# A two-layer graph network on one core: the order of the first loads, the dummy products, and the last result in three pieces

## The chip, the core and the metric

The kernel runs on one core of a Trainium2 chip. Five engines work beside each other, each through its own list of instructions in order: TensorE (PE in the profile, its weight loads PEld), VectorE (DVE), ScalarE (ACT), GpSimd (POOL) and SyncE (SP, which only issues transfers). ScalarE and GpSimd issue transfers too, each through its own queue. The metric is device microseconds of the whole program, and one number stands for a kernel: the median of several runs. All times below are in microseconds unless marked ns.

## The reference

Thirty-two graphs of 512 nodes with 128 features share one 512x512 adjacency of zeros and ones. Layer 0 is graph attention, layer 1 a gated recurrence of five steps; each is added to its input.

```python
h = jnp.maximum(_layernorm(x, axis=-1), 0.0)
x = x + _L0_gnn_ref(h, adj, W, b, a_src, a_dst)
h = jnp.maximum(_layernorm(x, axis=-1), 0.0)
x = x + _L1_gnn_ref(h, adj, adj, w3_w, ..., u5_b, 5)

# layer 0
h = einsum('bnf,fc->bnc', x, W)
logits = leaky_relu((h @ a_src)[:, :, None] + (h @ a_dst)[:, None, :], 0.2)
alpha = softmax(logits + mask, axis=-1)
out = leaky_relu(einsum('bij,bjc->bic', alpha, h) + b, 0.3)

# layer 1, one step (in_matrix and out_matrix are both adj)
m_in = einsum('nm,bmd->bnd', in_matrix, h);  m_out = einsum('nm,bmd->bnd', out_matrix, h)
av = concatenate([m_in, m_out], axis=-1);    u3 = h @ u3_w.T + u3_b
z = sigmoid(av @ w3_w.T + w3_b + u3);        r = sigmoid(av @ w4_w.T + w4_b + u3)
hv = tanh(av @ w5_w.T + w5_b + (r * h @ u5_w.T + u5_b))
h = (1.0 - z) * h + z * hv
```

## The kernel before

**A plan made on the host.** While the program is built, every piece of work becomes a `Task` with an engine, an estimated length, a key (its due time), the tasks that it needs, the buffers that it takes, and `lands`, the time until its result is seen. `plan` (L107) then walks through simulated time and picks for each engine the task with the lowest key among those that could begin, and the instructions are recorded in that order. So each engine's order is fixed by these estimates: `STORE_LANDS` and `SPREAD_LANDS` (L69) are the times allowed for a store or a load on GpSimd's queue, `CROSSED` (L70) the one for a transposing transfer, `ADJ_LANDS` (L38) the one for the adjacency. `SHIFT` (L48) moves single tasks' keys by parts of a step. `EARLY` and `LEVEL` (L35) say for how many graphs the pace of the due times differs at the start and at the end. `BRANCH` (L71) is how many tasks stand behind the load of a flag, which every engine reads to decide whether a general path has to run; here it never does.

**The first loads.** ScalarE's queue issues gw (the layer's 128x128 weight) and the two score vectors, one row each (L430 to L432). SP issues x of graph 0, the adjacency `a_sb` (1 MB), x of graphs 1 and 2, and the other weights (L449 to L454). TensorE turns gw (L476), multiplies the two score rows by a one to make columns of them (L487), and multiplies gw with these columns (L496). Four small ScalarE copies (L501 to L504) put the result beside gw into `wrow`, so that one product per tile (`hp`, L866) gives both the features and the scores.

**Dummies.** `idle` (L462) is a product of constants. Its tasks have a key behind everything, so the plan puts them where TensorE would have nothing else: the first `FIRST_IDLE` of 480 units from 500 ns on, the other `IDLE` of 256 units from 6500 ns on.

**Layer 0** of a graph: the norm's statistics and the relu on DVE, GpSimd and ScalarE; the turned activations (`h0T`, by TensorE for the first four graphs, later by 32x32 blocks on DVE and a trip through DRAM that GpSimd issues, L793 and L806); `hp`; exponentials of the scores on ScalarE; `es`, the scores of all nodes along the free axis; the weights `pt` (L981, DVE), which need `es` and a block of the transposed adjacency `adjT`; the averages `av` (L1013); the addition of x (`join`, L1066); and the second norm. `adjT` is made by TensorE turns (L527) and a copy per block (L534), block 3's on DVE (`BY_DVE`). Graph 3's `join` runs on GpSimd (`JOIN_POOL`).

**Layer 1.** Each state lives transposed (`hT`, times 4096) and as two f16 halves `hi` and `lo` with nodes on the partitions. A step on TensorE: eight f16 products with `adjT` (`m`, L1129), then five f32 products of 512 columns: g (L1148, L1149), z (L1169), v (L1192, L1193). Each f32 product stands in the profile as two records. ScalarE makes the tanh of each, DVE three combinations (L1206, L1212, L1215). The crossing to the next step (`crossed`, L1326): ScalarE casts `hT` to f16, DVE takes the rest, and SP issues a transposing transfer for each (L1340). The first step's `hT` comes by the DRAM trip (`turn_b`). Up to ten graphs are under way, which covers the crossing's latency with other graphs' products.

**The end.** The last four graphs' results are turned by TensorE. For the last two (`near`) the kept part is made ahead: graph 30's by ScalarE (`lowered`, L1219), DVE (`keep`, `gated_hv`) and GpSimd (`twice`, L1231). Graph 31's last step is `ending` (L1351), in `PIECES` of two 128-column tiles each: tanh, two DVE instructions, turns, the result, and a store per piece on the queue that `STORES` names. The constants `plus` and `minus` (0.5 and -0.5/4096 times the identity) are made but not used.

Of the kernel before, what the change touches and what calls it, by code (L numbers as in the profile page):

```python
# [15 lines left out]
P = 128  # L16
# [18 lines left out]
EARLY = 6  # L35
LEVEL = 9
EARLY_NORMS = ("a1", "a2", "a3", "b0")
ADJ_LANDS = 5600  # L38
HALVED = 1
BY_DVE = (3,)  # L40
JOIN_POOL = (3,)
LOW_POOL = ()
UNSCALED = 1
PIECES = (2, 2)
STORES = ('ACT', 'SP')
ENDING_KEY = 0
Z_AHEAD = 0
SHIFT = {  # L48
    ('adj', 2): 0.13, ('adj', 3): 1.0, (0, 1, 'step'): 3.5, (0, 12): 1.5, (1, 2, 'step'): -1.5,
    (1, 9): 1.85, (2, 0, 'step'): 3.0, (2, 1, 'step'): 1.5, (2, 15): 6.0, (2, 18): 1.0,  # L50
    (2, 2, 'step'): -0.08, (2, 9): -2.0, (25, 1, 'step'): 1.0, (25, 2, 'step'): -0.5,
    (25, 4, 'step'): -3.5, (26, 2, 'step'): 8.5, (27, 4, 'step'): -1.5, (29, 1, 'step'): 1.5,
    (29, 3, 'step'): -0.55, (29, 4, 'step'): -3.0, (3, 0): -0.5, (3, 0, 'step'): 1.0,
    (3, 15): 3.0, (3, 18): 5.5, (3, 26): 1.84, (3, 5): -3.0, (3, 9): -1.23, (30, 3, 'step'): -0.5,
    (30, 4, 'step'): -4.0, (31, 3, 'step'): -2.27, (4, 9): 2.0,
# [11 lines left out]
FIRST_IDLE, IDLE = 32, 36  # L67
LANDING = 5000
STORE_LANDS, SPREAD_LANDS = 3500, 5000  # L69
CROSSING, CROSSED = 1250, 1400  # L70
BRANCH = 150  # L71
# [236 lines left out]
def gat_then_gated_gnn_kernel(  # L308
# [40 lines left out]
    def add(*args, **kwargs):  # L349
        tasks.append(Task(*args, **kwargs))  # L350
        return tasks[-1]
# [53 lines left out]
    avecs = prep.tile([1, 2, D], F32, name="avecs")  # L405
# [3 lines left out]
    unlift = const.tile([P, 1], F32, name="unlift")  # L409
    nc.vector.memset(unlift, -1 / LIFT)  # L410
# [9 lines left out]
    def load_x(b, key=None, lands=3000):  # L420
        f = Buffer("x")

        def issue():
            pin(nc.sync.dma_start(out=new(f, f"x_{b}", (P, K, D)), in_=x_r[b]))

        needs = () if key else (bias_loaded,)
        load = add("SP", [1], key or 5 * (b - LEAD) * STEP, issue, needs, (f,), lands=lands)
        return f, load

    nc.scalar.dma_start(out=gw, in_=g_w)  # L430
    nc.scalar.dma_start(out=avecs[:, 0, :], in_=g_asrc.rearrange("(o d) -> o d", o=1))
    nc.scalar.dma_start(out=avecs[:, 1, :], in_=g_adst.rearrange("(o d) -> o d", o=1))  # L432
# [17 lines left out]
    a_loaded = add("SP", [1], -9.8e9, lambda: load_rest("a"), lands=ADJ_LANDS)  # L450
    xs[1] = load_x(1, -9.7e9, 5000)
    xs[2] = load_x(2, -9.6e9, 5100)
# [15 lines left out]
    for i in range(FIRST_IDLE + IDLE):  # L468
        add("PE", [480 if i < FIRST_IDLE else 256], 1e12, idle, (), (f_idle,),
            at=500 if i < FIRST_IDLE else 6500)  # L470
# [6 lines left out]
            at=4000)  # L477
# [6 lines left out]
    def issue():  # L484
        new(f_ac, "ac_ps")
        for i in range(2):
            pin(nc.tensor.matmul(  # L487
                f_ac.tile[:, i : i + 1], lhsT=avecs[0:1, i, :], rhs=ones[0:1, 0:1], start=True,
                stop=True,
            ))  # L490

    u = add("PE", [256] * 2, soon, issue, (), (f_ac,), at=4100)
    u = add("ACT", [1], soon, lambda: pin(nc.scalar.copy(acols, f_ac.tile[:, 0:2])), (u,), (f_ac,))

    def issue():
        pin(nc.tensor.matmul(new(f_wa, "wa_ps")[:, 0:2], lhsT=gwT, rhs=acols, start=True, stop=True))  # L496

    t = add("PE", [256], soon, issue, (u, t), (f_wa,), at=4800)

    def issue():  # L500
        pin(nc.scalar.copy(wrow[:, D : D + 1], f_wa.tile[:, 1:2]))  # L501
        pin(nc.scalar.mul(wrow[:, D + 1 : D + 2], f_wa.tile[:, 0:1], 0.8))
        pin(nc.scalar.mul(wrow[:, D + 2 : D + 3], f_wa.tile[:, 1:2], -0.8))
        pin(nc.scalar.copy(wa, f_wa.tile[:, 0:2]))  # L504
# [318 lines left out]
    def layer0(b):  # L823
# [7 lines left out]
        def keys(i):  # L831
            return begin + length * (base[0] + i) / parts + SHIFT.get((b, base[0]), 0) * STEP
# [168 lines left out]
        def o():  # L1001
            return f_o.tile or new(f_o, f"o_{b}", (P, K, D))
# [63 lines left out]
        def join(ks):  # L1066
            pin((nc.gpsimd if by_pool else nc.vector).tensor_tensor(x1[:, ks, :], f_x.tile[:, ks, :], o()[:, ks, :], ALU.add))

        by_pool = False
        if by_halves:  # L1070
            joined = []
            for part, ks in enumerate((slice(0, K // 2), slice(K // 2, K))):
                t = add("DVE", [256], keys(0.3 * part), lambda ks=ks: leak(ks), averaged[part : part + 1],
                        (f_o,))
                joined.append(add("DVE", [256], keys(0.3 * part), lambda ks=ks: join(ks), (t,),
                                  (f_o, f_x)))
        else:
            t = add("DVE", [512], keys(0), lambda: leak(slice(0, K)), averaged, (f_o,))
            by_pool = b in JOIN_POOL
            joined = [add("POOL" if by_pool else "DVE", [512], keys(0), lambda: join(slice(0, K)),  # L1080
                          (t, finished.get(b - SLOTS)), (f_o, f_x), ns=1350 if by_pool else None)]
# [13 lines left out]
    def halves(b, src, key, needs, buffers, order="p k d -> p k d", **sizes):  # L1095
        hi = his[b % SLOTS].rearrange(order, **sizes)
        lo = los[b % SLOTS].rearrange(order, **sizes)

        def low():
            pin((nc.gpsimd if by_pool else nc.vector).tensor_tensor(lo, src(), hi, ALU.subtract))  # L1100

        by_pool = b in LOW_POOL

        high = add("ACT", [480], key, lambda: pin(nc.scalar.copy(hi, src())), needs, buffers)
        return high, add("POOL" if by_pool else "DVE", [512], key, low, (high,), buffers,
                         ns=1350 if by_pool else None)


    def recurrence(b, step, halved, turned):
# [109 lines left out]
        def lowered():  # L1219
            pin(nc.scalar.activation(  # L1220
                new(f_kept, f"less_{b}"), f_z.tile, AF.Identity, bias=unlift, scale=1 / LIFT
            ))

        def keep():
            pin(nc.vector.tensor_tensor(new(f_d, f"kept_{b}"), f_kept.tile, hT, ALU.mult))
# [5 lines left out]
        def twice():  # L1231
            pin(nc.gpsimd.tensor_tensor(f_d.tile, f_hv.tile, f_d.tile, ALU.subtract))

        if near:
            f_kept = Buffer("r")
            t_keep = add("ACT", [512], keys(4), lowered, (t_z,), (f_z, f_kept))
            t_keep = add("DVE", [512], keys(3.5) - STEP, keep, (t_keep,), (f_kept, f_d))
            t = add("DVE", [512], keys(5), gated_hv, (t, t_z), (f_z, f_hv))
            turned = add("POOL", [512], keys(5), twice, (t, t_keep), (f_hv, f_d), ns=1400)
            to_turn = f_d  # L1240
        else:
            t = add("DVE", [512], keys(5), differ, (t,), (f_hv, f_d))
            t = add("DVE", [512], keys(5), gated, (t, t_z), (f_z, f_d))
            turned = add("DVE", [512], keys(5), update, (t,), (f_d,))
            to_turn = None
# [66 lines left out]
        def result_at_once():  # L1312
            pin(nc.vector.scalar_tensor_tensor(
                new(f_res, f"res_{b}", (P, K, D)), src(), 0.5 if near else 1 / LIFT,
                x1s[b % SLOTS], ALU.mult, ALU.add,
            ))
# [34 lines left out]
    def ending(b, keys, t_rh, t_z, buffers):  # L1351
# [13 lines left out]
        def piece(i, ks):  # L1365
            f = Buffer("o", "bank") if i else f_v
            of = slice(ks.start * P, ks.stop * P)
# [14 lines left out]
            def gated():  # L1382
                hv = f_hv.tile[:, of]
                pin(nc.vector.scalar_tensor_tensor(
                    hv, f_z.tile[:, of], 1.0, hv, ALU.add, ALU.mult
                ))
                pin(nc.vector.scalar_tensor_tensor(
                    f_d.tile[:, of], hv, LIFT, f_d.tile[:, of], ALU.mult, ALU.subtract
                ))

            def turn():
                for k in range(ks.start, ks.stop):
                    pin(nc.tensor.transpose(
                        f.tile[:, ts(k - ks.start, P)], f_d.tile[:, ts(k, P)], ident
                    ))

            def result():
                res = f_res.tile or new(f_res, f"res_{b}", (P, K, D))
                pin(nc.vector.scalar_tensor_tensor(
                    res[:, ks, :], f.tile[:, :width].rearrange("p (k d) -> p k d", d=D),  # L1400
                    0.5 / LIFT, x1s[b % SLOTS][:, ks, :], ALU.mult, ALU.add,
                ))
# [10 lines left out]
            u = add("DVE", [width] * 2, keys(4 + key), gated, (u, t_z, t_keep), (f_z, f_hv, f_d))  # L1413
            u = add("PE", [256] * (ks.stop - ks.start), keys(4 + key), turn, (u,), (f, f_d))
            u = add("DVE", [width], keys(5 + key), result, (u,), (f, f_res))
# [66 lines left out]
```

## Time and profile before

| | us |
|---|---|
| median of 5 runs | 1138.51 |
| lowest and highest | 1136.83, 1139.75 |
| profiled execution, its time | 1137.72 |
| profiled execution, its span | 1136.0 |
| TensorE busy in it | 1127.9 |
| DVE, ACT, POOL busy | 874.2, 666.7, 359.9 |

The span runs from the program's first instruction to its last. The time of an execution is 1.7 longer than its span. A product of 512 columns in f32 is recorded as two matmuls of 592 ns, which start 429 ns apart when they follow each other, and one in f16 as one of 379 ns with 216 ns to the next; so records overlap, and where one asks what TensorE was held up by, the distance from start to start says more than the busy time.

### The profile page before, as it was taken

The numbers are of one execution on the slowest core, as the hardware profiler recorded it, in microseconds if no ns is written. First come the engines' busy times: TensorE is split into PE (matmuls) and PEld (weight loads), VectorE is DVE, ScalarE is ACT, GpSimd is POOL, SyncE is SP. The second block draws the span as 40 slices with busy tenths as digits, with TensorE's granted clock in tenths as the row PEclk, the third lists the DMA queues.
The fourth block names the chain that finished last, engine by engine and source line by source line (L and its number), as shares of the span: only waits on it lengthen the run. The fifth ranks groups of instructions, "written<-read, shape, count | busy, mean of one in ns | idle before, by whom it ended". The sixth has DMA issues, their size and how long they took to land.

```text
span 1136.0 us, 14339 instructions
## 1 busy us (share of the span) xinstructions
PE 1127.9 (99%) x4318; PEld 591.1 (52%) x4318; DVE 874.2 (77%) x2007; ACT 666.7 (59%) x1302; POOL 359.9 (32%) x516
## 2 busy tenths in 40 slices
PE   9999999999999999999999999999999999999998
PEld 7555554555455544555544555555555554444444
DVE  7978868787777778787787887798887976647555
ACT  6666656555655566565566565666665555545553
POOL 4446614331430344322344322545453130100000
DMA  3345526464435446444455444555564343322222
GB/s 107 75 103 112 111 57 112 88 125 84 108 82 95 97 106 108 90 92 107 93 108 100 88 100 107 102 121 113 111 121 87 63 93 56 74 47 70 69 65 68
DMA packets 188629, 105.56 MB, mean 93 GB/s; under 512 B 152066, under 2 KB 167556, under 8 KB 188420
## 3 DMA queue, kind: packets, MB, share of 16 engines
q1 hardware_dynamic: 170368, 66.57, 25.9%
q0 software_dynamic: 17888, 37.84, 18.3%
q8 instruction: 35, 0.57, 0.2%
q14 instruction: 46, 0.38, 0.1%
q10 hardware_dynamic: 292, 0.20, 0.1%
HBM read 39.98 MB, written 30.99 MB: 62 GB/s over the span
## 4 chain that ended last, share of the span: by engine, by line
PE 93%; DVE 3%; DMA 2%; ACT 1%; POOL 1%; issue 1%; ACTq 0%; DVEq 0%; POOLq 0%
PE m L1129 23%; PE g L1148 12%; PE g L1169 12%; PE g L1149 12%; PE v L1193 11%; PE v L1192 11%; PE av L1013 9%; PE hp L866 2%; DVE pt L981 1%; DMA turn_b<-blocks_b 1%; DMA hi<-hiT 0%; PE idle L463 0%; DMA hT<-turn_b 0%; DMA avecs<-in_L_gnn_a_dst_dram 0%; DVE st_a L656 0%
## 5 line engine op out<-in xcount | busy, mean ns | idle before, releaser
L1206 DVE SCALAR_TENSOR_TENSOR d<-hv,hT 128x512 f32<-128x512 f32 x158 | 108.4, 686 | 112.5 <-ACT hv L1199 111.7
L1154 ACT ACTIVATE rs<-g,zrb 128x512 f32<-128x512 f32 x160 | 109.9, 687 | 119.3 <-PE g L1149 117.6
L1199 ACT ACTIVATE hv<-v,vb 128x512 f32<-128x512 f32 x159 | 108.9, 685 | 116.2 <-PE v L1193 115.9
L1148 PE MATMUL g<-hT,u3T 128*128 128x512 f32 x320 | 163.6, 593 | 1.1 <-DMA hT<-turn_b 1.1
L1129 PE MATMUL m<-adjT,hi 128*128 128x512 f16 x640 | 162.9, 379 | 1.7 <-DMA hi<-hiT 1.7
L1149 PE MATMUL g<-mT,w4sT 128*128 128x512 f32 x320 | 163.4, 592 | 0.0
L1169 PE MATMUL g<-mT,w3dT 128*128 128x512 f32 x320 | 162.5, 592 | 0.0
L1192 PE MATMUL v<-mT,w5sT 128*128 128x512 f32 x318 | 162.4, 592 | 0.0
L1193 PE MATMUL v<-rh,u5hT 128*128 128x512 f32 x318 | 162.4, 592 | 0.0
L1129 PE MATMUL m<-adjT,lo 128*128 128x512 f16 x640 | 162.0, 379 | 0.0
L1161 DVE SCALAR_TENSOR_TENSOR rh<-rs,hT 128x512 f32<-128x512 f32 x160 | 109.5, 686 | 53.1 <-ACT rs L1154 48.8
L685 POOL TENSOR_TENSOR rs_b<-ve_b,mhalf 128x4 f32<-128x4 f32 x32 | 37.5, 1173 | 349.4 <-DVE ve_b L665 209.6
L1181 ACT ACTIVATE zs<-g,zrb 128x512 f32<-128x512 f32 x160 | 109.8, 686 | 62.1 <-PE g L1169 61.6
L1013 PEld LDWEIGHTS av<-hw,pt 128*128 128x128 f32 x1024 | 124.4, 191 | 23.4 <-issue 18.7
L1140 ACT COPY mT<-m 128x512 f32<-128x512 f32 x160 | 93.3, 584 | 73.0 <-PE m L1129 70.4
L1013 PE MATMUL av<-hw,pt 128*128 128x129 f32 x1024 | 126.1, 275 | 0.2 <-DVE pt L981 0.2
L1332 ACT CAST hiT<-hT 128x512 f16<-128x512 f32 x128 | 78.8, 616 | 72.1 <-DVE hT L1215 72.0
L1215 DVE SCALAR_TENSOR_TENSOR hT<-d,hT 128x512 f32<-128x512 f32 x158 | 109.3, 692 | 13.0 <-PE v L1192 0.5
L1129 PEld LDWEIGHTS <-hi 128*128 128x128 f16 x640 | 62.5, 98 | 106.0 <-issue 52.8
L1212 DVE SCALAR_TENSOR_TENSOR d<-zs,d 128x512 f32<-128x512 f32 x158 | 109.3, 692 | 5.2
L1129 PEld LDWEIGHTS <-lo 128*128 128x128 f16 x640 | 62.4, 98 | 91.0 <-issue 24.9
L1149 PEld LDWEIGHTS g<-mT,w4sT 128*128 128x128 f32 x320 | 60.8, 190 | 76.5 <-issue 70.8
(148 smaller groups left out, 1384.2 us busy)
## 6 DMA issues: line engine op xcount, KB each, us to landing
x<-in_x_dram SPq DMA_DIRECT2D x32, 256.0 KB, 2.9
out_dram<-res SPq DMA_DIRECT2D x31, 256.0 KB, 2.2
turn_b<-blocks_b POOLq DMA_DIRECT2D x120, 64.0 KB, 2.8
hT<-turn_b POOLq DMA_DIRECT2D x30, 256.0 KB, 3.6
turn_a<-blocks_a POOLq DMA_DIRECT2D x112, 64.0 KB, 2.9
h0T<-turn_a POOLq DMA_DIRECT2D x28, 256.0 KB, 3.7
es<-line POOLq DMA_DIRECT2D x28, 256.0 KB, 4.2
way<-blocks SPq DMA_DIRECT2D x28, 256.0 KB, 2.0
```

The lines of the kernel that those rows point to most:

```text
L1013: pin(nc.tensor.matmul(avs()[:, i, :], lhsT=f_pts[c].tile[:, ts(2 * part + i, P)], rhs=hw()[:, c, : D + 1], start=start, stop=(c == K - 1) ...
L1129: pin(nc.tensor.matmul(f_m.tile, lhsT=part[:, k, :], rhs=adjT[:, k, :], start=(first and k == 0), stop=(not first and k == K - 1),))
L1148: pin(nc.tensor.matmul(g, lhsT=u3T, rhs=hT, start=True, stop=False))
L1149: pin(nc.tensor.matmul(g, lhsT=w4sT, rhs=f_mT.tile, start=False, stop=True))
L1154: pin(nc.scalar.activation(new(f_r, f"rs_{b}_{step}"), f_g.tile, AF.Tanh, bias=rb, scale=0.5))
L1161: pin(nc.vector.scalar_tensor_tensor(new(f_rh, f"rh_{b}_{step}"), f_r.tile, 1.0, hT, ALU.add, ALU.mult))
L1169: pin(nc.tensor.matmul(f_g.tile, lhsT=w3dT, rhs=f_mT.tile, start=False, stop=True, skip_group_check=True))
L1181: pin(nc.scalar.activation(new(f_z, f"zs_{b}_{step}"), f_g.tile, AF.Tanh, bias=zb, scale=0.5))
L1192: pin(nc.tensor.matmul(v, lhsT=w5sT, rhs=f_mT.tile, start=True, stop=False))
L1193: pin(nc.tensor.matmul(v, lhsT=u5hT, rhs=f_rh.tile, start=False, stop=True))
L1212: pin(nc.vector.scalar_tensor_tensor(d, f_z.tile, 1.0, d, ALU.add, ALU.mult))
L1215: pin(nc.vector.scalar_tensor_tensor(hT, f_d.tile, 0.5, hT, ALU.mult, ALU.add))
```

## The change

- The score vectors become two partitions of one tile, are loaded ahead of gw on ScalarE's queue, and are turned by one TensorE transpose. The product with gw gets each column 32 times (64 columns, 32 of each score).
- SP loads x of graph 1 ahead of the adjacency.
- All adjacency blocks are copied by ScalarE; no join is on GpSimd.
- 24 + 32 dummies where there were 32 + 36; the second kind is shorter in the plan (190 units) and may begin at 5500.
- Graph 30's kept part is made by DVE alone.
- Graph 31's result comes in pieces of 2, 1 and 1 tiles, stored by SP, ScalarE, ScalarE. The first piece (`BY_MATMUL`) is turned by products with `minus` (the kept part, early) and `plus` (the gated part) that add up in PSUM.
- Estimates, `SHIFT`, `EARLY`, `LEVEL` and `BRANCH` are others, and with them the order of all engines. In TensorE's order of the new kernel the 56 dummies stand among the start's products, the last one in graph 0's second step, and none after it; in the old one 33 stand in the start and 35 among the last products.

```diff
-EARLY = 6
-LEVEL = 9
+EARLY = 7
+LEVEL = 8
-ADJ_LANDS = 5600
+ADJ_LANDS = 5650
-BY_DVE = (3,)
-JOIN_POOL = (3,)
-LOW_POOL = ()
+BY_DVE = ()
-PIECES = (2, 2)
-STORES = ('ACT', 'SP')
-ENDING_KEY = 0
+PIECES = (2, 1, 1)
+STORES = ('SP', 'ACT', 'ACT')
+ENDING_KEY = -4
+BY_MATMUL = (0,)
 SHIFT = {
...
-FIRST_IDLE, IDLE = 32, 36
+FIRST_IDLE, IDLE = 24, 32
-STORE_LANDS, SPREAD_LANDS = 3500, 5000
+STORE_LANDS, SPREAD_LANDS = 4000, 5500
-BRANCH = 150
+BRANCH = 110
...
-    avecs = prep.tile([1, 2, D], F32, name="avecs")
+    avecs = prep.tile([2, D], F32, name="avecs")
...
+    nc.scalar.dma_start(out=avecs[0:1, :], in_=g_asrc.rearrange("(o d) -> o d", o=1))
+    nc.scalar.dma_start(out=avecs[1:2, :], in_=g_adst.rearrange("(o d) -> o d", o=1))
     nc.scalar.dma_start(out=gw, in_=g_w)
-    nc.scalar.dma_start(out=avecs[:, 0, :], in_=g_asrc.rearrange("(o d) -> o d", o=1))
-    nc.scalar.dma_start(out=avecs[:, 1, :], in_=g_adst.rearrange("(o d) -> o d", o=1))
...
-    a_loaded = add("SP", [1], -9.8e9, lambda: load_rest("a"), lands=ADJ_LANDS)
-    xs[1] = load_x(1, -9.7e9, 5000)
-    xs[2] = load_x(2, -9.6e9, 5100)
+    xs[1] = load_x(1, -9.8e9, 3700)
+    a_loaded = add("SP", [1], -9.7e9, lambda: load_rest("a"), lands=ADJ_LANDS)
+    xs[2] = load_x(2, -9.6e9, 6000)
...
-        add("PE", [480 if i < FIRST_IDLE else 256], 1e12, idle, (), (f_idle,),
-            at=500 if i < FIRST_IDLE else 6500)
+        add("PE", [480 if i < FIRST_IDLE else 190], 1e12, idle, (), (f_idle,),
+            at=500 if i < FIRST_IDLE else 5500)
...
-        for i in range(2):
-            pin(nc.tensor.matmul(
-                f_ac.tile[:, i : i + 1], lhsT=avecs[0:1, i, :], rhs=ones[0:1, 0:1], start=True,
-                stop=True,
-            ))
+        pin(nc.tensor.transpose(new(f_ac, "ac_ps")[:, 0:2], avecs, ident[0:2, 0:2]))
...
-        def lowered():
-            pin(nc.scalar.activation(
-                new(f_kept, f"less_{b}"), f_z.tile, AF.Identity, bias=unlift, scale=1 / LIFT
-            ))
         def keep():
-            pin(nc.vector.tensor_tensor(new(f_d, f"kept_{b}"), f_kept.tile, hT, ALU.mult))
+            pin(nc.vector.scalar_tensor_tensor(
+                new(f_d, f"kept_{b}"), f_z.tile, -1.0, hT, ALU.add, ALU.mult
+            ))
...
         def twice():
-            pin(nc.gpsimd.tensor_tensor(f_d.tile, f_hv.tile, f_d.tile, ALU.subtract))
+            pin(nc.vector.scalar_tensor_tensor(
+                f_d.tile, f_hv.tile, LIFT, f_d.tile, ALU.mult, ALU.subtract
+            ))
...
+            def turn_kept():
+                new(f_end, f"end_{b}_{i}")
+                for k in range(ks.start, ks.stop):
+                    pin(nc.tensor.matmul(
+                        f_end.tile[:, ts(k - ks.start, P)], lhsT=f_d.tile[:, ts(k, P)], rhs=minus,
+                        start=(k == ks.start), stop=False, skip_group_check=True,
+                    ))
+
             def turn():
                 for k in range(ks.start, ks.stop):
-                    pin(nc.tensor.transpose(
-                        f.tile[:, ts(k - ks.start, P)], f_d.tile[:, ts(k, P)], ident
-                    ))
+                    if by_matmul:
+                        pin(nc.tensor.matmul(
+                            f_end.tile[:, ts(k - ks.start, P)], lhsT=f_hv.tile[:, ts(k, P)],
+                            rhs=plus, start=False, stop=True, skip_group_check=True,
+                        ))
+                    else:
+                        pin(nc.tensor.transpose(
+                            f.tile[:, ts(k - ks.start, P)], f_d.tile[:, ts(k, P)], ident
+                        ))
...
+            n = ks.stop - ks.start
+            if by_matmul:
+                kept = add("PE", [512] * n, keys(-1), turn_kept, (t_keep, pieces[0]), (f_end, f_d))
+                u = add("DVE", [width], keys(4 + key), gated, (u, t_z), (f_z, f_hv))
+                u = add("PE", [512] * n, keys(4 + key), turn, (u, kept), (f_end, f_hv))
+            else:
+                u = add("DVE", [width] * 2, keys(4 + key), gated, (u, t_z, t_keep),
+                        (f_z, f_hv, f_d))
+                u = add("PE", [256] * n, keys(4 + key), turn, (u,), (f, f_d))
+            u = add("DVE", [width], keys(5 + key), result, (u,), (f_end, f_res))
```

## The prediction

> **What bounds the kernel now.** I read the busy line first, then the chain of waits over the whole span, the waits by engine, the busy time by stretches, and at last the chain and the timeline of both ends.
>
> ```profile
> PE 1127.9 (99%) x4318; PEld 591.1 (52%) x4318; DVE 874.2 (77%) x2007; ACT 666.7 (59%) x1302; POOL 359.9 (32%) x516
> ...
> PE 93%; DVE 3%; DMA 2%; ACT 1%; POOL 1%; issue 1%; ACTq 0%; DVEq 0%; POOLq 0%
> ```
>
> TensorE is the bound, but busy time counts filling instructions, so I asked for stretches:
>
> ```profile
> 0.00:26.00 26.00, 24.09 (x181) 20.88 (x182) 19.69 (x93) 17.29 (x56) 9.59 (x24) 1.00 0.35 117
> 60.00:340.00 280.00, 280.00 (x1057) 145.75 (x1057) 223.37 (x521) 168.80 (x331) 107.75 (x151) 1.00 0.49 98
> 352.00:1094.00 742.00, 742.00 (x2751) 380.59 (x2751) 570.74 (x1257) 432.29 (x822) 222.13 (x316) 1.00 0.44 92
> 1126.00:1136.00 10.00, 6.70 (x50) 5.29 (x48) 4.92 (x9) 1.48 (x3) 1.26 (x1) 1.00 0.18 58
> ```
>
> After the window come its length and the busy time of PE, weight loads, DVE, ACT, POOL. From 60 to 340 and from 352 to 1094 TensorE has not one gap, and both kernels put the same products there. The change can win or lose only in the first 60 us, in single stalls, and in the last 10 us. The stalls are two:
>
> ```profile
> PE m L1129 <- DMA hi<-hiT: 1.7, 1, 1.7
> PE g L1148 <- DMA hT<-turn_b: 1.1, 1, 1.1
> ```
>
> By start-to-start distances, longer than a pair's usual 0.43 and 0.22, they cost 1.82 us at 52.5 and 1.29 us at 347.6. The ends:
>
> ```profile
> 1.77 4.40 DMA avecs<-in_L_gnn_a_dst_dram
> ...
> 6.21 0.38 PE ac_ps L487 x2
> ```
>
> ```profile
> 1126.48 1.26 POOL L1232 TENSOR_TENSOR kept<-hv,kept 128x512 f32<-128x512 f32 x1 [137.64 <-DVE hv L1229]
> 1126.57 1.73 DVE L1359 SCALAR_TENSOR_TENSOR kept<-zs,hT 128x512 f32<-128x512 f32 x1 [0.17 <-ACT zs L1181]
> ...
> 1130.85 0.38 ACTq L1406 DMA_DIRECT2D out_dram<-res  x1
> 1131.18 1.51 SPq L1406 DMA_DIRECT2D out_dram<-res  x1
> ```
>
> At the start a 512-byte row of the score vectors takes 4.40 us and holds TensorE until 6.21. At the end a DVE instruction that takes 0.69 elsewhere takes 1.73 beside GpSimd's, the last issue on SP takes 1.51 against 0.33 of its like, and the span ends 4.8 us after that issue began.
>
> **The start.** The ScalarE queue issued at 0.74, 1.26 and 1.77. The score rows now take the first two places and gw the third. The third row took 4.40 because it came behind the adjacency's 8 KB packets, whose records run from 3.1 to 5.6; gw in the first place took 3.2. So gw lands between 1.77 + 3.2 = 4.9 and 1.77 + 4.4 = 6.2. I take 4.9: x of graph 1 (256 KB) now goes ahead of the adjacency, which at the 390 GB/s of these packets puts off the adjacency by 0.67, to begin near 3.7, while gw's packets, 1.66 after the issue as in the old first place, come at 3.43. From gw on: turn to copy 0.45, copy 0.27, product and four copies as from 6.87 to 7.61, 0.74, so wrow is whole at 6.4, not 7.61. The adjacency lands at 6.36 + 0.67 = 7.0, and its first turn, at 7.96 before since it stood behind wrow's work, starts at 7.05. The two score columns cost one transpose for two products, nothing beside the wait.
>
> What follows is ScalarE and DVE. ScalarE now casts the fourth adjacency block too (BY_DVE empty; 0.6 more on ScalarE, 0.68 less on DVE, nothing else). From its first cast's end, 7.05 + 0.68 + 0.59 = 8.32, stand the exponentials 0.80, scaling 1.15, two casts 1.20, two relus 0.8 and the fourth cast 0.6: 12.9. The two last weighings at 0.415 end at 13.7; they ended at 14.54. From there to the bias of graph 1's second norm (33.41) DVE worked 18.87 us; the new order has one mean and variance pair and one small product less on this stretch (0.7). So this bias comes 0.8 to 1.5 us earlier, and the first aggregation of graph 1 with it, with the same TensorE work before it (26.4 us of products by pitch in both orders). If gw lands late, only DVE's 0.7 is left, or nothing. I take -1.1, bounds -1.5 and 0.
>
> Of the dummies (0.11 each) 56 now lie in the start and none at the end; before it was 33 and 35. Eighteen run during the first load. The 22 that are new, 2.4 us, stand where TensorE waits for ScalarE's copies and DVE's weighings; that wait is their cover, and without it they cost up to +2.4. I take 0. Without dummies in the end, the turns of the last pieces follow each other within 0.9 us, as the 0.76 and 0.22 us gaps there do now.
>
> The clock column above reads 1.00 in every stretch, but the dummies' own rows do not: 0.213 us apart up to 4.36, 0.11 from 6.5 on. The Trainium skill, TensorE: Matmul & The Clock Gate, section Part 1: The HAM clock gate, says that an idle window of about 3.4 us halves the clock. By it the end without dummies would stay at full rate, its gaps being shorter, and at half rate the six turns would cost 0.11 more each, 0.7; no trace here shows such a gap.
>
> Against the new place of gw speaks DMA: Bandwidth & Descriptors, section Queues, rings and completion order: an engine drains a whole packet of one queue's descriptors before it turns to the next queue. The row agrees (the late row moved at 5.40, when the adjacency was nearly through). By the rule everything hangs on which comes first, and coming second would make the start's term -0.7 or less.
>
> **The ramp and its crossings.** Each step's state goes from TensorE's v over ScalarE, three DVE steps, a cast and SP's transposing DMA back to m. I added the pitches of the products that stand between in each order. Before, graph 1 step 1 had 7.8 us and needed 9.78: the stall of 1.82. Needed in the ramp: 7.45 to 10.4, the contended two 9.78 and 9.68; after 1000 us: 6.3 to 6.7. The new order gives 7.4 (graph 4 step 3), 8.0 (1, 1), 8.6 (0, 2), 8.8 (0, 1), 8.8 (3, 1), where the old gave 7.8, 8.3, 8.8, 9.1, and 10.4 for (3, 1). At most 1.8 is saved; if (3, 1) and (4, 3) wait 0.9 and 1.0 more, it is +1.9. Nearest is the old row for (1, 1) again with a little more for (3, 1): +0.3. Late, the least is 7.7, as before, where the slack was 1.0 to 1.5; there the flag's load (0.55 on DVE, 0.47 on ScalarE, 0.51 on SP) now stands beside graph 29 step 4's crossing with a slack of 1.48: 0, without that slack +0.5.
>
> **The turn_b stall.** The plan now puts a POOL store 0.5 us later and a POOL load 0.5 later, so first steps are placed 1.0 later against their state's arrival. The old slacks of this arrival were 0.04, 0.11, 0.31 at the worst; the 1.29 shrinks to about 0.3. I take -0.9; bounds -1.3 and, for another late landing of the same kind (2.2 to 6.4 us), +1.0. Joining graph 3 on DVE costs 0.69 of an engine that is idle 23%.
>
> **The end.** ScalarE's lowering (0.72, hidden before it waited for v) goes. GpSimd's 1.26 goes, and DVE does it in 0.69. DVE from 1125.71: three full instructions 2.07, one half 0.41, the result of graph 30 0.69, two quarters at about 0.28 (halving the step from 0.69 to 0.41) 0.56, a half result 0.41, two quarters 0.56, a quarter result 0.28; then the last quarter waits for its turn 0.58 after its input, and takes 0.28: 1131.27, with the overlap the rows show (0.62 apart, not 0.69) 1130.9. Before: 1131.15. The arithmetic saves nothing; the instructions that three pieces add eat what GpSimd held up. The stores gain: 64 KB are left at the last issue, not 128, and graph 30's 256 KB leave at 1128.9, not 1130.5. A store by itself landed 2.0 us after its issue (1119.3, 1123.1), the last two 3.6. So between +0.2 and -1.7; I take -0.8, since an instruction fetch of 1.37 us at 1130.94 lay across them, and what fetches at the program's end is unchanged. The two turns by products with plus and minus cost 0.44 more of an idle TensorE.
>
> **Sum.** -1.1 + 0.3 - 0.9 - 0.8 = -2.5. The profiled execution took 1137.72 (span 1136.0, 1.7 around it), which gives 1135.2; the median of the runs is 0.79 higher, and moved by as much gives 1136.0, my forecast. About 0.2%, 2.3 us, is what a measurement here can tell.
>
> **Rivals.** Hidden anyway: gw comes behind the adjacency (for it: the old third row; against it: the 0.2 us by which it is ahead), the ramp waits for the same casts, the last store meets the fetch again: only DVE's 0.7 is left, 1137.8. Slower: the ramp's crossings, as contended as (1, 1) and (3, 1) were, all need 9.7 us: shortfalls 2.3 + 1.7 + 1.1 + 0.9 + 0.9 + 0.2 = 7.1 less the 2.0 there now, +5.1; an earlier start is then only a longer wait, the end and turn_b keep -1.7: 1141.9. It decides from 4.0 us of new stalls on. For it: less TensorE work between. Against it: crossings (0, 1) and (0, 2) needed 7.45 and 8.8.
>
> **Numbers.** Forecast 0.52, all of it counted as faster, own range 1133.5 to 1137; hidden anyway 0.26, the same; slower crossings 0.22. Below 1133 or above 1141.5 I leave 0.15.
>
> **What would show it.** wrow's copies done by 6.6 and the first weighing before 10.2; no TensorE gap over 1 us near 347 or in its place; m's waits for hi before 100 us, 1.5 to 3 us in all; the last result at 1.1 us or less before the last store's issue, and that store landing in 2.0 to 3.6. Wrong if gw lands after 6, or if crossings stall over 4 us.

## The result, and the profile after

The changed kernel is slower: 1140.9 us, median of 25 runs, against 1138.87 of 47 runs of the kernel before; the ratio is 1.0018 with a 95% interval of 1.0011 to 1.0025, some 2.0 us. The forecast was 1136.0. The profiled execution after took 1139.76 (span 1137.9), before 1137.72 (span 1136.0), each 1.1 below its median, so the two profiles differ by as much as the medians and can be set beside each other.

The page after, first the busy line, then the chain that ended last:

```profile
PE 1127.3 (99%) x4313; PEld 593.2 (52%) x4313; DVE 871.5 (77%) x2009; ACT 665.1 (58%) x1303; POOL 359.7 (32%) x514
...
PE 97%; DMA 1%; DVE 0%; issue 0%; ACT 0%; SPq 0%
```

TensorE is as busy as it was. The chain has lost DVE's 3% and POOL's 1%, which looks like progress; it only says that fewer of TensorE's waits ended on them. TensorE's own waits of over 1 us, in us in all, number of times, and the longest:

```profile
PE at_ps L524 <- DMA a_sb<-in_adj_dram: 2.8, 1, 2.8
PE m L1122 <- DMA lo<-loT: 1.8, 1, 1.8
```

Both such waits of before (`hi` 1.7, `turn_b` 1.1) are gone and two others stand in their place: one on the adjacency at the start, which did not exist, and one on a `lo`.

To see where time went I took each product at its own start-to-start pitch (0.429 for an f32 record of 512 columns, 0.216 for an f16 one, 0.11 for short ones), without dummies, and subtracted their running sum from the clock. That **lost time**, when so much useful work is done, in us (the last column is the time from the first z product of graph 31 to the end of the span):

| useful work done | 6 | 26 | 60 | 240 | 340 | 1110 | end |
|---|---|---|---|---|---|---|---|
| before | 7.3 | 9.3 | 11.5 | 11.5 | 12.9 | 12.5 | 11.2 |
| after | 10.9 | 13.2 | 13.9 | 15.8 | 15.8 | 16.2 | 9.8 |

So the start loses 3.6 in its first 6 us of work, the ramp wins back 1.5 between 26 and 60, a new stall costs 2.0 before 240, the old one at 340 is gone (-1.4), 0.8 more goes between 340 and 1110 in waits of under 0.4 each, and the end is 1.3 shorter. (Lost time can't really fall: 12.9 to 12.5 says that the pitches taken are a little long, in both rows alike.) Three rows of the start before, then the timeline of the start after (start, length, engine, what; in brackets the idle time before and what ended it):

```profile
7.96 0.64 PE L527 MATMUL at_ps<-ident,a_sb 128*128 128x128 f32 x4
8.44 1.06 PE L866 MATMUL hp<-wrow,h0T 128*128 128x131 f32 x8
10.71 1.66 DVE L981 SCALAR_TENSOR_TENSOR pt<-es,hw,adjT 128x256 f32<-128x256 f32 x4
```
```profile
1.61 0.39 ACTq L430 DMA_DIRECT2D gw<-in_L_gnn_W_dram  x1
1.66 0.48 SPq L434 DMA_DIRECT2D a_sb<-in_adj_dram  x1
...
4.65 0.27 PE L474 MATMUL gwT_ps<-ident,gw 128*128 128x128 f32 x1
...
5.92 0.18 ACT L501 COPY wa<-wa_ps 128x2 f32<-128x2 f32 x1
...
9.77 0.75 PE L524 MATMUL at_ps<-ident,a_sb 128*128 128x128 f32 x4 [2.83 <-DMA a_sb<-in_adj_dram]
10.36 1.52 PE L863 MATMUL hp<-wrow,h0T 128*128 128x131 f32 x8
...
13.20 1.70 DVE L978 SCALAR_TENSOR_TENSOR pt<-es,hw,adjT 128x256 f32<-128x256 f32 x4 [0.67 <-PE es L923]
```

gw and `wrow` are early, at 4.65 and 6.10, better than forecast. But the adjacency, issued at 1.66, is there only at 9.7; TensorE stands still for 2.83, and the eight `hp` then take 1.52 where they took 1.06 before. The granted clock shows half rate there (window, its length, busy time of PE, weight loads, DVE, ACT, POOL, clock, DMA share, GB/s):

```profile
6.90:9.70 2.80, 0.04 (x1) 0.00 (x0) 0.16 (x2) 0.00 (x0) 2.26 (x4) 1.00 0.82 301
9.70:14.30 4.60, 4.53 (x25) 4.48 (x26) 2.83 (x15) 2.90 (x10) 1.85 (x4) 0.63 0.30 63
```

0.63 is the mean of a stretch of 3.41 us at half rate, from 10.80 on. The first weighing starts at 13.20, 2.5 later than the 10.71 of before, where the forecast had it before 10.2.

The second new wait, on the chain around 250 us (start, length, what):

```profile
247.35 2.17 PE m L1122 x11
249.52 4.84 DMA lo<-loT
...
254.41 1.04 PE m L1122 x4
```

This `lo` needs 4.84 from its issue; the median for all 128 of its kind is 2.5. GpSimd's four `turn_a` stores (issued from 248.31, landed by 254.11) are under way beside it, and `line` stores behind them.

The end:

```profile
1132.92 0.33 SPq L1414 DMA_DIRECT2D out_dram<-res  x1
...
1133.65 1.51 ACTq L1414 DMA_DIRECT2D out_dram<-res  x2
1133.90 0.29 DVE L1407 SCALAR_TENSOR_TENSOR res<-v_end,x 128x128 f32<-128x128 f32 x1 [0.28 <-PE v_end L1401]
```

The last piece's store is issued at 1134.22, as the last result ends, as foreseen; the end of the span, at 1137.9, is 3.7 later (before: last issue at 1131.18, 4.8 ahead of the end).

### The profile page after: what moved, and what is told of

The parts are those of the page before. It is cut to its first block, busy times and chain, and to the rows that moved or that the text cites. A ratio compares the mean times of both kernels' runs of the same rounds, so it can differ in the third digit from the quotient of the medians.

```text
span 1137.9 us, 14292 instructions
## 1 busy us (share of the span) xinstructions
PE 1127.3 (99%) x4313; PEld 593.2 (52%) x4313; DVE 871.5 (77%) x2009; ACT 665.1 (58%) x1303; POOL 359.7 (32%) x514
## 4 chain that ended last, share of the span: by engine, by line
PE 97%; DMA 1%; DVE 0%; issue 0%; ACT 0%; SPq 0%
PE m L1122 24%; PE g L1142 12%; PE g L1141 12%; PE g L1162 12%; PE v L1185 12%; PE v L1186 12%; PE av L1010 10%; PE hp L863 2%; DMA a_sb<-in_adj_dram 1%; DMA lo<-loT 0%; DMA hi<-hiT 0%; PE at_ps L524 0%; PE idle L461 0%; PE es L923 0%; PE t_a L755 0%
## 5 line engine op out<-in xcount | busy, mean ns | idle before, releaser
L1208 DVE SCALAR_TENSOR_TENSOR hT<-d,hT 128x512 f32<-128x512 f32 x158 | 109.2, 691 | 12.4
```

Source lines behind the costliest of these rows:

```text
L1208: pin(nc.vector.scalar_tensor_tensor(hT, f_d.tile, 0.5, hT, ALU.mult, ALU.add))
```

## Experiments

Times are medians in us of 12 runs, ratios are to the kernel before on the same chip (its median there: 1139.06 for e1 to e4, 1139.12 for e5 to e8, 1139.98 for e9 to e11, 1139.70 for e12 to e15). Since the medians of the kernel before differ by 0.9 from chip to chip, ratios are compared, and medians only within a group. A profile is one execution.

**e1 to e4: which half of the load order.** e1 has no edit. e2:

```diff
-    xs[1] = load_x(1, -9.8e9, 3700)
-    a_loaded = add("SP", [1], -9.7e9, lambda: load_rest("a"), lands=ADJ_LANDS)
+    a_loaded = add("SP", [1], -9.8e9, lambda: load_rest("a"), lands=ADJ_LANDS + 430)
+    xs[1] = load_x(1, -9.7e9, 3700 - 430)
```

e3:

```diff
+    nc.scalar.dma_start(out=gw, in_=g_w)
     nc.scalar.dma_start(out=avecs[0:1, :], in_=g_asrc...)
     nc.scalar.dma_start(out=avecs[1:2, :], in_=g_adst...)
-    nc.scalar.dma_start(out=gw, in_=g_w)
```

e4 is the first edit the other way round in the kernel before (x of graph 1 at -9.8e9, the adjacency at -9.7e9).

> The changed kernel itself, unchanged. Theory (the order of loads makes the adjacency late, TensorE stands still and runs at half rate after it): the first turn of the adjacency again starts past 9 us (9.77 in the profile after, 7.96 before), a run of products 0.21 apart instead of 0.11 follows it, and the mean granted clock is again 0.996 to 0.999. Rival (one transfer had bad luck in one execution): the first turn starts near 7.1, the clock is 1.000, and the two microseconds are somewhere else. Both expect 1.0018 of the kernel before.

> The changed kernel with one thing undone: x of graph 1 is issued behind the adjacency again, as in the kernel before; the landing times that the plan is told are moved by the same amount, so that the orders of TensorE, VectorE and ScalarE stay as they are. Theory: the adjacency lands near 6.4 to 6.8, its first turn starts by 7.1, no product is at half rate after it, the start is 2.5 to 4 us shorter and the time falls from 1140.9 to 1137 to 1138.5. Rival (the ramp waits for its casts and crossings whatever the start does): the start is shorter by as much, but stalls of m on hi of 2 us or more come back in the ramp, and the time stays within 0.7 us of the changed kernel's. Rival (bad luck of one profile): nothing changes, 1140.9.

> The changed kernel with the other half of the loads undone: on ScalarE's queue gw is issued first again and the score rows second and third; every engine's order but this stays. Theory (x of graph 1 ahead of the adjacency is what delays the adjacency): its first turn still starts past 9 us and the time stays at 1140.9 within 0.7. Rival (the 128 packets of gw, which now move at 3.5 to 3.75 just as the adjacency begins, delay it): the first turn starts by 7.5, and the time falls by 2 us or more.

> The kernel before with only this: x of graph 1 issued ahead of the adjacency, the plan's landing times moved so that the orders of TensorE, VectorE and ScalarE stay. Theory: the first turn of the adjacency, 7.96 before, starts past 9, and the time rises by 1.5 to 4 us, to 1.0013 to 1.0035 of the kernel before. Rival (the adjacency only moves by the 0.7 that 256 KB take): the first turn stays at 8.0 since it stands behind other work anyway, and the time is the same within 0.5 us.

| | time | ratio | 95% | first turn of the adjacency |
|---|---|---|---|---|
| e1 changed kernel again | 1140.87 | 1.0012 | 0.9997-1.0028 | 9.80 |
| e2 adjacency ahead again | 1140.48 | 1.0010 | 1.0001-1.0020 | 9.94 |
| e3 gw ahead again | 1136.81 | 0.9987 | 0.9975-0.9998 | 7.16 |
| e4 before, x of graph 1 ahead | 1138.84 | 0.9999 | 0.9985-1.0012 | 8.21 |

My theory, that x of graph 1 ahead of the adjacency was the harm, fell: doing only that costs nothing (e4), undoing it helps nothing (e2). Its rival for e3 held: with gw first the whole loss is gone: 4.1 us between the medians of e3 and e1 on the same chip, 2.8 by the ratios, and eight of e3's twelve runs are faster than every one of e1's. The late adjacency of the profile after was not one execution's accident, since e1 shows it again. The issues of loads by line, KB, and us to landing; first e1, then e3, then e2:

```profile
a_sb<-in_adj_dram SPq DMA_DIRECT2D x1, 1024.0 KB, 8.1
gw<-in_L_gnn_W_dram ACTq DMA_DIRECT2D x1, 64.0 KB, 3.0
```
```profile
a_sb<-in_adj_dram SPq DMA_DIRECT2D x1, 1024.0 KB, 5.4
gw<-in_L_gnn_W_dram ACTq DMA_DIRECT2D x1, 64.0 KB, 3.3
```
```profile
a_sb<-in_adj_dram SPq DMA_DIRECT2D x1, 1024.0 KB, 5.5
gw<-in_L_gnn_W_dram ACTq DMA_DIRECT2D x1, 64.0 KB, 5.3
```

In e3 the adjacency lands at 7.04, which is the 7.0 of the forecast. With gw in the third place one of the two is late: the adjacency (e1), or, when that goes ahead, gw (e2: it lands at 6.9 and TensorE waits 1.78 for it). In e2 the adjacency is there by 6.7 and its first turn still comes at 9.94:

```profile
6.97 0.34 PE L474 MATMUL gwT_ps<-ident,gw 128*128 128x128 f32 x1 [1.78 <-DMA gw<-in_L_gnn_W_dram]
...
8.66 1.49 PE L461 MATMUL idle<-const-bfloat16-1.0 128*128 128x256 bf16 x6
9.94 1.06 PE L524 MATMUL at_ps<-ident,a_sb 128*128 128x128 f32 x4
```

Six dummies stand ahead of it in TensorE's order and, at half rate (from 8.28 to 11.7), take 1.28. So a dummy in the in-order list can hold up work that is ready.

**e5 to e8: gw second, and three other terms.** e5 issues gw between the two score rows. e6 to e8 stand on e3. e6, besides: 

```diff
-    (4, 2, 'step'): 5.64,
+    (4, 2, 'step'): 5.0,
```

e7, besides: `PIECES = (2, 2)`, `STORES = ('ACT', 'SP')`, `ENDING_KEY = 0`, `BY_MATMUL = ()`. e8, besides, records nothing for the 32 later dummies.

> The changed kernel with ScalarE's queue in the order score row, gw, score row: gw is issued near 1.36, between its 0.74 in the last arrangement that was fast and its 1.61 in the changed kernel. Theory (what counts is whether gw's 128 packets are through before the adjacency's first packets at 3.6 to 3.8): they move at about 3.0 to 3.5, the adjacency lands by 7.1, its first turn starts by 7.3, and the time is that of the run with gw ahead, 0.9975 to 0.9998 of the kernel before. Rival (a score row ahead of gw is enough to hold up the adjacency, whatever gw's time): its first turn starts past 9 us and the time is 1.0005 to 1.0025.

> gw ahead again, and one more edit: the shift of graph 4's step 2 from 5.64 to 5.0, which places this step's products one place earlier, so that 10.85 us of products, not 8.24, stand between the end of step 2 and the first product that takes lo of step 3. All four profiles of the changed plan show a stall of 2.01 to 2.07 there, near 250 us. Theory (the crossing of lo, slowed by GpSimd's stores of the same moment, is that stall): it goes, the lost time between 236 and 240 us of useful work rises by less than 0.4 instead of 2.0, and the time falls by 1.5 to 2.1 us against the run with gw ahead: 1134.5 to 1135.5, 0.996 to 0.9975. Rival (the crossing is late whenever it is issued, or its wait moves on to another product): at least 1.2 us of the stall stands at another place within 20 us, and the time is that of the run with gw ahead.

> gw ahead again, and the last result in two halves as in the kernel before, stored from ScalarE's and SP's queues, without the products with plus and minus; graph 30's kept rows stay on VectorE. The prediction gave the end -0.8 in all. Theory (three pieces shorten the stores at the end): from the first z product of graph 31 to the end it takes 0.5 to 1.2 longer than the 10.64 of the run with gw ahead, and the time is 0.3 to 1.2 higher. Rival (the extra instructions eat the gain, and taking GpSimd out was all of it): the end takes 10.64 within 0.4 and the time is the same.

> gw ahead again, and the 32 later dummies left out of the program, every other instruction in its place; the 24 of the first load stay. The prediction took the 22 new ones at 0, with a bound of 2.4. Theory (they stand where TensorE waits anyway): the lost time at 26 us of useful work is 9.16 within 0.3, the time within 0.5 of the run with gw ahead, if no stretch runs at half rate. Rival (they push products back): lost time and time fall by 0.8 or more. Third way (without them TensorE stands still long enough for the clock to fall): a stretch with products 0.21 apart shows before 30 us, and the time is 1 us or more higher.

| | time | ratio | 95% | lost at 6 | 26 | 60 | 240 | 1110 | end |
|---|---|---|---|---|---|---|---|---|---|
| e3 | 1136.81 | 0.9987 | 0.9975-0.9998 | 6.9 | 9.2 | 9.9 | 12.6 | 12.6 | 10.6 |
| e5 | 1139.88 | 1.0001 | 0.9985-1.0016 | 10.0 | 12.2 | 12.8 | 14.6 | 15.9 | 10.7 |
| e6 | 1136.48 | 0.9978 | 0.9962-0.9993 | 7.2 | 9.4 | 10.2 | 10.1 | 11.1 | 9.9 |
| e7 | 1137.79 | 0.9987 | 0.9974-1.0001 | 9.4 | 11.6 | 12.4 | 14.3 | 15.1 | 10.8 |
| e8 | 1137.32 | 0.9984 | 0.9970-0.9997 | 6.7 | 8.2 | 9.6 | 11.6 | 13.5 | 10.7 |

e5: the first turn starts at 10.11, as the rival said. The theory's premise failed too, since gw's packets moved at 3.6 in the median although gw was issued second. The time lies between the two, unclear.

e6: the stall near 250 us is gone, and did not move on:

```profile
PE m L1122 <- DMA lo<-loT: 0.8, 1, 0.8
```

is the only wait on a `lo` left, and it stands at 1099 us, at graph 29's step 4, beside the flag's load. That the stall was the crossing of `lo`, with too few products before it, is shown. That GpSimd's stores made it so is not: in e6 this `lo` meets none and takes 2.4 from its issue at 240.86, but it is issued later, needs 10.6 in all (10.2 in the profile after), and has 10.85 us of products before it. Of the expected 1.5 to 2.1 us the ratios show 0.0009, 1.0 us, with intervals that overlap, so what the stall is worth in the time is not settled. e6 is faster than both kernels: 1136.48, 2.6 below the kernel before on its chip.

e7: the end takes 10.8 against 10.6, within the rival's bounds, and the ratio is e3's. The profiled execution met a late adjacency although gw was first (landing 7.8 after its issue), and how many of the other eleven did is not known, so the time says little about the end.

e8: neither theory. Without the later dummies 1.0 less is lost at 26, so they do push products back; 0.8 of it is given back at a `lo` near 65 us, and 1.3 at 1099, and the time is e3's. After 5 us nothing ran at half rate before the last product.

**e9 to e11: is it gw's packets?** e9 takes gw to SP's queue, right behind x of graph 0; e10 is e9 with the shift of e6; e11 has both halves of the loads as before (e2 and e3 together).

> The changed kernel with gw issued on SP's queue, right behind x of graph 0, and the two score rows alone on ScalarE's; every engine's order of work stays. x of graph 1 and the adjacency are issued 0.43 later for it. Theory (gw's 128 packets from a second queue, moving at 3.5 to 4.1 as the adjacency's begin, hold up some engine's share of the adjacency; from the same queue they pass ahead of it): gw's packets are through by 3.3, the adjacency's last packet ends at 6.9 to 7.4 instead of 9.3 to 9.7, its first turn starts by 7.7, and the time is 1136 to 1138, as with gw ahead. Rival (gw's place is not the cause, the adjacency is late by chance or for the score rows): its last packet still ends past 9 and the time is 1139.5 or more.

> gw on SP's queue as in the run beside it, and the step 2 of graph 4 one place earlier, which took the stall near 250 us away in an earlier run. If both causes are what they seemed and add up, the lost time at 600 us of useful work is 10.0 to 10.8 (12.77 in the profile before, 15.70 after), and the time is 1134.5 to 1136.5, below both kernels. Rival (an earlier start or one stall less is given back at a later crossing): the time is within 0.7 of the run beside it.

> The changed kernel with all its loads issued in the order of the kernel before: gw, score row, score row on ScalarE's queue, the adjacency ahead of x of graph 1 on SP's. Theory: the adjacency lands near 6.4 and gw near 4.1, as in the kernel before, the last score row near 5.4 to 5.7; the turn of both rows waits for it and holds TensorE behind it, so wrow is whole at 7.0 to 7.7, and the time is 1136.5 to 1138.5. With the three other arrangements this fills a square of two by two: gw ahead would be worth 3 to 4 us whether or not x of graph 1 goes ahead. Rival (only the pair that moves together harms): the time is above 1139.

| | time | ratio | 95% | last packet of the adjacency | first turn |
|---|---|---|---|---|---|
| e9 | 1138.65 | 0.9984 | 0.9972-0.9997 | 8.34 | 8.75 |
| e10 | 1138.04 | 0.9984 | 0.9970-0.9998 | 9.42 | 9.84 |
| e11 | 1139.02 | 0.9991 | 0.9978-1.0003 | 6.14 | 9.90 |

The times say that gw off the third place of ScalarE's queue mends it again. The packets say that gw's own transfer beside the adjacency isn't needed to hold it up: in e9 and e10 it passed on the same queue by 3.3 and 3.5, and the adjacency is late all the same. e10 adds nothing to e9, against the expectation; its profile has a late start of 13.3 lost at 26, and the stall near 250 is gone in it as in e6 (13.9 lost at 60, at 240 and at 340). e11's first turn is late for e2's reason: the last score row is there at 6.2, and half rate begins at 7.1. It fills the square: gw first is worth 0.0025 and 0.0019 in the two orders of SP's queue (1.0012 and 0.9987; 1.0010 and 0.9991), and SP's order shows nothing in either. The second pair is from two chips and its intervals overlap, so by itself it proves little; in their profiles the first turn is as late in e11 as in e2.

**e12 to e15: rows or gw, and the kernel before.** e12 leaves gw alone on ScalarE's queue and issues the score rows on SP's, behind x of graph 0. e13 puts one more load of gw, into a tile nothing reads, ahead of the rows. e14 is the edit of e3 the other way round in the kernel before, and nothing else; e15 is e14 and e4 together.

> The changed kernel with gw alone on ScalarE's queue, issued at 0.74, and the two score rows on SP's queue right behind x of graph 0, so that x of graph 1 and the adjacency are issued some 0.6 to 0.9 later; all orders of work stay. So far the adjacency's 128 packets that took over 400 ns were 8 to 24 of them in the six profiles with the score rows first, 1 to 5 in the seven with gw first. Theory A (gw's transfer early on the second queue keeps the adjacency's packets short): 6 or fewer long packets, the last one ends by 7.7, the time is 1136.5 to 1138.5. Theory B (the score rows ahead of the large loads are the harm, on whichever queue): 8 or more long packets, the last ends past 8.3, the time is over 1138.5.

> The changed kernel with one more transfer: the 64 KB of gw are also loaded into a tile that nothing reads, in the first place of ScalarE's queue, ahead of the score rows; gw itself comes fourth, issued near 2.2. Theory A (an early transfer of 128 packets on the second queue is what matters): 6 or fewer of the adjacency's packets take over 400 ns, its last one ends by 7.2; gw may land as late as 6.9 behind it. Theory B (gw late, or the rows, make the packets long): 8 or more, the last ends past 8.3. In both the time is 1139 or more, since gw is late.

> The kernel before with only ScalarE's queue in the order of the changed kernel: score row, score row, gw; the adjacency stays ahead of x of graph 1. If the queue's order by itself is what costs, as the pairs of runs on the changed plan say (2.2 to 4 us): gw lands near 6.5 to 6.9 instead of 4.1, wrow is whole past 8.3 instead of 7.61, and the time is 1.001 to 1.003 of the kernel before. Rival (the stall of 1.82 that the old plan has at 52 us takes up what the start loses): the time is within 0.0007 of the kernel before.

> The kernel before with all the loads in the order of the changed kernel: score rows first, x of graph 1 ahead of the adjacency. If the late adjacency belongs to this pair of orders: its last packet ends past 8.3, 8 or more packets take over 400 ns, the first turn starts past 9 (7.96 before) and the time is 1.0015 to 1.004 of the kernel before; then the rest of the change, plan and ending, gains what is missing to 1.0018. Rival (the lateness came from the changed plan): last packet by 7.2, the same time within 0.0007.

| | time | ratio | 95% | adjacency: last packet, packets over 400 ns | gw: last packet |
|---|---|---|---|---|---|
| e12 | 1138.55 | 0.9994 | 0.9980-1.0007 | 9.60, 11 | 3.4 |
| e13 | 1141.65 | 1.0020 | 1.0005-1.0036 | 7.40, 4 | 8.1 |
| e14 | 1142.25 | 1.0020 | 1.0004-1.0036 | 5.87, 11 | 6.6 |
| e15 | 1142.56 | 1.0022 | 1.0007-1.0036 | 8.83, 21 | 8.2 |

e14 is the plainest run of the study: three lines in another order make the kernel before slower by 0.0020, 2.3 us, as much as the whole change did. Its gw took, from issue to landing (3.2 before):

```profile
gw<-in_L_gnn_W_dram ACTq DMA_DIRECT2D x1, 64.0 KB, 5.4
```

TensorE stands still for 2.59 until it lands and runs at half rate until 12.28; the first weighing starts at 14.36, where it was 10.71. This profile (1145.49) is 3.2 above e14's median, for it also waited 3.7 for `turn_b`, a stall that differs from run to run in the old plan (0.0 to 4.9). What TensorE waited for in e15:

```profile
PE gwT_ps L476 <- DMA gw<-in_L_gnn_W_dram: 4.5, 1, 4.5
PE g L1148 <- DMA hT<-turn_b: 2.0, 1, 2.0
PE m L1129 <- DMA hi<-hiT: 1.7, 1, 1.7
```

Theory A fails on e12 (gw early and first, long packets all the same), theory B on e13 (rows ahead of gw, short ones). One pattern is left over all 17 profiles: where ScalarE's queue begins with a score row, 8 to 24 of the adjacency's 128 packets take over 400 ns (eight profiles), where it begins with gw or its copy and the rows follow, 1 to 5 (eight); e12, with gw alone on that queue, has 11. What inside the DMA engines makes the packets long is not settled.

With these runs both plans stand in all four orders of the loads (ratios to the kernel before):

| | gw first, adjacency ahead | gw first, x of graph 1 ahead | rows first, adjacency ahead | rows first, x of graph 1 ahead |
|---|---|---|---|---|
| old plan | 1 | 0.9999 (e4) | 1.0020 (e14) | 1.0022 (e15) |
| new plan | 0.9991 (e11) | 0.9987 (e3) | 1.0010 (e2) | 1.0012 (e1), 1.0018 (after) |

Single steps are within or near the noise, but the four pairs agree: rows ahead of gw cost 0.0019 to 0.0031 each time (2.2 to 3.5 us), SP's order makes 0.0008 at most, and the new plan with its ending gains 0.0004 to 0.0012 (0.5 to 1.4 us).

## Why the prediction was wrong

**The step that failed** is "The adjacency lands at 6.36 + 0.67 = 7.0", as far as it took gw's move to the third place at nothing for the adjacency. In both profiles of the changed kernel TensorE had it only at 9.8. The reckoning of bytes ahead was right where gw is first: with x of graph 1 ahead the adjacency landed at 7.04, 7.08, 7.30 and 6.91 (e3, e4, e6, e8). I had asked of gw's third place only when gw itself would land, and that part was right: gw's turn at 4.65, `wrow` whole at 6.10 where 6.4 was forecast, and gw's packets through at 4.06, when the adjacency's had just begun (3.79). So the sign that I had named for being wrong, gw after 6, did not show; the first weighing, to be before 10.2, came at 13.20. Gaining the score rows' 1.2 us at the price of gw's place cost another load more: with gw third, gw or the adjacency was late in all five profiles (after, e1, e2, e14, e15), with gw first and the rows behind it on the same queue in one of seven (e7; not in before, e3, e4, e6, e8, e11). That the order does it is shown by the times of e1 and e3 and of e14; by what path inside the DMA engines stays open.

The term of -1.1 became +3.6. TensorE stands still for 2.83 and then runs at half rate for 3.41; e1, whose adjacency is as late but whose clock stayed up, had lost 9.6 by 6 us of work, after 10.9, e3 6.9. So, against e3, some 2.7 are the late adjacency and some 1.3 the half rate. Nor does the -1.1 come back with gw first: e3 has lost 9.2 at 26, before 9.3. It is there in e8 alone (8.2), so the later dummies use up what the loads gain.

**The rival "hidden anyway"** named gw behind the adjacency, and priced it at 1137.8 as a gain missed. In e2 and e14 just that happened, and it costs about 2 us: 2.3 in e14, and 2.2 in e2 against e11, with intervals that overlap. The price left out what is queued behind gw's turn on TensorE: the copies to `wrow`, the turns of h, the dummies and the adjacency. In e14 gw lands 3.1 later than before, and the first weighing starts 3.7 later.

**The rival "slower"** named 1141.9, near what was measured, but by m's waits on `hi` in the ramp, and the new plan has no such stall there: the nearness is luck.

**The ramp.** I took +0.3 by "the old row for (1, 1) again". The old stall of 1.82 there stands in all four profiles of the old plan (1.97 to 2.03 lost between 40 and 50) and in none of the new one, with 0.2 more products before it: its `hi` takes 5.00 before, beside GpSimd's stores from the first to the last, and 3.54 in e3, where the last of four lands at 51.37, so this crossing needs 8.13 in e3, not 9.78. Instead (4, 3), which I gave up to 1.0, costs 2.0, and not by `hi` but by the `lo` behind it, which I had not counted: it needed 10.2, and 8.24 us of products stand before it. Need is a matter of what else runs and moves at that moment, not of the crossing's number: over the profile after, transposing transfers that met no `turn_a` or `turn_b` store took 2.44 in the median (122 of those whose landing is known), those that shared over 1.5 us with such stores 4.75 (50).

**turn_b.** Right, and too small: the new plan has no such stall in any of 13 profiles. In the old plan it was 1.4, 0.0, 4.9 (with half rate behind it) and 2.3 in four (before, e4, e14, e15); the one I priced was one draw of these.

**The end.** -0.8 was forecast. From the first z of graph 31 it took 9.7 to 10.8, mean 10.35, in twelve profiles with three pieces, and 10.7 to 11.2, mean 10.84, in the four of the old ending: -0.5. e7 could not tell pieces from GpSimd.

**The dummies** were taken at 0: right for the time (e8), though not for the reason given. They do push back products by 1.0, which is what the start would have gained, and without them later waits take it back. Late in the kernel a flag's load was taken at 0 or +0.5; the stall beside it was 0 to 1.3 in the new plan's profiles.

**The end's arithmetic.** The pieces listed for DVE's last stretch add up to 1131.55; 1131.27 leaves out one quarter result. The forecast did not use it: the -0.8 came from the stores.

**The sum.** With gw's place put right (e3) the ratio is 0.9987, -1.5 us against the -2.5 of the forecast. That it comes so near is partly luck. The start gives nothing instead of -1.1; the plan and the ending, for which ramp, turn_b and end were to give -1.4, give 0.5 to 1.4 in the four pairs, but by other crossings than forecast. What put the changed kernel behind the kernel before is the one load order.

## What to carry to other kernels

When loads change places, follow each of them to its landing, and not only the one that is to come earlier: on a start bound by loads, the last one decides, and moving a short wait off it can put a longer one in its place. Here the 64 KB weight belonged first on its queue, and the two 512-byte rows behind it. Before tuning a plan's due times by single stalls, look at several executions: the stalls at 52 us (old plan) and near 250 (new plan, until its step was moved) stood in every profile, but the late loads, the `turn_b` stall and the one at 1099 came and went.

## What the runs showed of the hardware

The adjacency's 128 packets of 8 KB take 309 ns each, most of the time. In some executions 8 to 24 of them took 0.4 to 2.1 us, on several engines in the same moment (in e10 eight that began between 6.8 and 7.1 ended between 7.9 and 8.6), or, as the ends and beginnings fit together, one engine began its eight only at 5.3 or 5.9 and ended past 9 (e7, e1). Bytes ahead of a transfer, which I had reckoned with, give the landing of the quiet executions (7.04 in e3 for 7.0) and not of these.

Once full rate had been reached, half rate came in stretches of 3.41 us or twice that, but a gap's length does not decide it alone: TensorE stood still for 1.78 and fell (e2), for 2.83 and fell (after), for 2.54 and did not (e12). So the prediction's reading, that gaps shorter than 3.4 us keep the full rate, is not borne out by itself; at the end, where the gaps are under 1 us, no profile of the new plan has half rate before the last product. The Trainium skill, TensorE: Matmul & The Clock Gate, section Part 1: The HAM clock gate, says that the activity window runs freely and that the same kernel may start at different phases of it. The traces agree: the changed kernel reached full rate at 4.0 us in one execution and at 5.8 in another (after, e1).
